# Layer 0's first-layer sums: two points in one VectorE operation, with interleaved pairs from ScalarE

## The chip, the cores and the metric

The kernel runs on one core of a Trainium2 chip. Its time is the device time of one execution in microseconds (us); lower is better. A core has TensorE (PE, the matmuls), VectorE (DVE), ScalarE (ACT), GpSimd (POOL) and SyncE (SP), each with its own queue of instructions, and 16 DMA engines that they share. All data here are float32.

## The reference

Four layers run one after the other on images of 512 channels; only layer 0 is touched by the change. It is an attention with 8 groups, whose keys are sampled at 64 learned offsets per group, and whose scores get a bias from a small network (the "continuous position bias"), for each pair of one of the 32x32 pixels and one of the 64 sampled points:

```python
pos = grid_q[:, :, None, :] - grid_kv[:, None, :, :]
bias = jnp.sign(pos) * jnp.log1p(jnp.abs(pos))
bias = jax.nn.relu(bias @ cpb_w1 + cpb_b1)       # 2 -> 128
bias = jax.nn.relu(bias @ cpb_w2 + cpb_b2)       # 128 -> 128
bias = (bias @ cpb_w3 + cpb_b3)                  # 128 -> 1
sim = jnp.einsum('bhid,bhjd->bhij', qh, kh) + bias
attn = jax.nn.softmax(sim, axis=-1)
```

There are 2 images x 8 groups x 64 points = 1024 points, and each has 1024 pixels. The first layer is separable: its input for pixel (y, x) has one part that depends on x alone and one that depends on y alone. So `relu(wx * X[x] + b + wy * Y[y])` is one sum of two rows of 32 numbers, spread over the 32x32 pixels and cut off at zero.

## The kernel before

Layer 0 (`layer0`, lines 192 to 963) works on eight tiles t of 128 (two groups of 64 points each). Inside a tile, 32 steps of four points: 256 steps i in all, one loop that is written out at build time. Four slots k make up a step. In each slot, one of the four parts of the second layer (32 of 128 outputs) is done for the step's four points.

What one step does, engine by engine:

- VectorE, `first(p)` (line 588; the operation is recorded at L599): the first layer of one point. A custom operation adds a row of 32 (the point's x part, from table `tab0`) and a column of 32 (its y part, from `tab1`) and cuts the sum off at zero; the result is 128 x 1024. It goes to `ring`, 11 buffers of one point each, three of their own (`h1`) and eight in the memory `wa` that later layers' weights use. Sums run `AHEAD = 7` points ahead of the step.
- PE, `second(i, h1s, part)` (L616): for each of the two halves of the pixels and the four points one matmul of 128 x 32 weights, which writes 32 of the 128 rows of a PSUM tile `z`. In the trace each such matmul has two records, 64 records to a step. The `z` tiles rotate through three buffers (`zt`, pool `att_ps_z`), which all other small PSUM tiles of the loop (`gpb`, `pk`, `pkv`, `pvo`, `po`, `pt`, `pa`, `pp`) share.
- ScalarE, in `second` (L625): bias and relu of `z` into an `h2` buffer: pool `h2q` (three buffers) for parts 1 and 3, `h2b` (three) for part 2, `h2p` or `h2j` (memory `bridge` and others) for part 0.
- VectorE, `joined` (L630): adds two parts into one, twice per step, in slots 1 and 3.
- GpSimd and SP: DMAs that add the joined parts of different rows into each other (L918 to L937), and the loads of the tables (L573).
- PE, `third` (L645) and `scores` (L653): every 16 steps, the third layer and the scores into `sim`.

The tables: `load_tabs(c)` (line 561) loads for a chunk c of 16 points the two 16x32 tables, one per axis, to all 128 partitions, from two buffers each (`tab0`, `tab1`). `scale_tab(c, ax)` (line 582) multiplies each with the first layer's weights, in place: on ScalarE at L587, on VectorE at L585 for the first chunk alone. In the loop that happens in steps with i % 4 = 1, the first axis in slot 0 and the second in slot 2, for the chunk that is needed a step later.

A chain of generators, `behind`, is advanced once in slots 1 and 3: the end of the tile before (`finish`: softmax, transposes, output projection), the offsets of the tile after next (`offsets`: on ScalarE 36 products at L408, reductions on VectorE at L414, a Gelu, L438, a Tanh), and the next tile's samples (`samples`: `gpb` L497, `near` L505 and L506, `wx` and `wy` L512 to L521, the matmuls `pk`, then `kvbd` L534, `pkv`, and `pvo` with the weights `ow`, which L492 loads together with `xt`, L488).

The order of the work is that of the program: `in_order` (line 57) ties each engine's instructions in layer 0 to the order in which they are written. A DMA stands on the queue that issues it. An instruction that waits holds up all that is behind it on its engine.

Of the kernel before, what the change touches and what calls it, by code (L numbers as in the profile page):

```python
# [19 lines left out]
P = 128  # L20
# [59 lines left out]
def kernel(ctx: ExitStack, tc: tile.TileContext, a: dict, out: bass.AP):  # L80
# [111 lines left out]
    def layer0(l0, fold_d, t2_b, o2_b):  # L192
# [6 lines left out]
        h2q = l0.enter_context(tc.tile_pool(name="att_h2q", bufs=3))  # L199
# [36 lines left out]
        ring = [one.tile([P, HW], F32, name=f"h1{k}") for k in range(3)]  # L236
        ring += [qkv2.rearrange("p k n -> p (k n)")[:, k * HW : (k + 1) * HW] for k in range(6)]
        ring += [proj2.rearrange("p k n -> p (k n)")[:, k * HW : (k + 1) * HW] for k in range(2)]
# [13 lines left out]
        ones = one.tile([P, P], F32, name="ones")  # L252
        nc.gpsimd.memset(ones, 1.0)
# [33 lines left out]
        def bias_weights():  # L287
            sort = h2b.tile([P, 7, P], F32, name="sort", tag="h2")
            row, below, w2t = [sort[:, k, :] for k in range(3)]
            perm = sort[:, 3:, :].rearrange("p b (r u) -> p b r u", u=32)  # L290
# [194 lines left out]
        def samples(t):  # L485
# [5 lines left out]
            ow = one.tile([P, C], F32, name="ow")  # L491
            nc.sync.dma_start(out=ow, in_=a["out_w"][pr * P : (pr + 1) * P, :])  # L492
# [18 lines left out]
            wx = one.tile([P, P], F32, name="wx")  # L511
# [15 lines left out]
            accumulate(pk[:, 1, :], [(wsum[:, 2:3].to_broadcast([P, P]), ident)])  # L527
            yield
            shift = one.tile([P, P], F32, name="shift")
# [12 lines left out]
            kq = one.tile([P, P], F32, name="kq")  # L542
# [3 lines left out]
            values = one.tile([P, P], F32, name="values")  # L546
# [16 lines left out]
        def load_tabs(c):  # L563

            t, rc = divmod(c, NCH)
            assert t in tables
            tabs_of[c] = []
            for ax in range(2):
                src = slog_d[t, ax].rearrange("(q r) i -> q r i", q=4)
                tab = two.tile([P, 16, 32], F32, name=f"tab{ax}")  # L570
                if 4 * c < LAST:
                    q, r = rc % 4, rc // 4 * 16
                    nc.sync.dma_start(out=tab, in_=src[q, r : r + 16, :].partition_broadcast(P))  # L573
                else:
                    q, r = rc % 2 * 2, 16 + (rc - 4) // 2 * 8
                    nc.sync.dma_start(
                        out=tab.rearrange("p (q r) i -> p q r i", q=2),
                        in_=src[q : q + 2, r : r + 8, :].partition_broadcast(P),
                    )
                tabs_of[c].append(tab)  # L580

        def scale_tab(c, ax):
            tab, w = tabs_of[c][ax], col("cpb_w1", ax)
            if c == 0:
                nc.vector.tensor_scalar(tab, tab, w, 0.0 if ax else col("cpb_b1"), ALU.mult, ALU.add)  # L585
            else:
                nc.scalar.activation(tab, tab, AF.Identity, bias=0.0 if ax else col("cpb_b1"), scale=w)  # L587

        def first(p):

            chunk, point = divmod(p, 16)
            if point == 0:
                tabs_of.pop(chunk - 1, None)
                if chunk + 1 < NT * NCH:
                    load_tabs(chunk + 1)
            tx, ty = tabs_of[chunk]
            h1 = ring[p % len(ring)]

            nc.vector._custom_dve(  # L599
                TENSOR_ADD_SAT,  # L600
                out=h1.rearrange("p (y x) -> p y x", x=W),
                in0=tx[:, point, :].unsqueeze(1).to_broadcast([P, H, W]),
                in1=ty[:, point, :].unsqueeze(2).to_broadcast([P, H, W]),
                s0=float(np.finfo(np.float32).max),
                s1=0.0,
            )
            return h1

        def second(i, h1s, part):

            z = zt([P, HW], "z")
            lo = BLOCK[part]
            for half in range(2):
                n = slice(half * HALF, (half + 1) * HALF)
                for point in range(4):
                    nc.tensor.matmul(  # L616
                        z[point * 32 : point * 32 + 32, n],
                        cpb_w2[:, lo : lo + 32],
                        h1s[point][:, n],
                        start=True,  # L620
                        stop=True,
                    )
            ring = h2q if part % 2 else h2b if part else h2j if i % (4 if i < LAST else 2) else h2p
            h2 = ring.tile([P, HW], F32, name="h2", tag="h2") if ring in (h2q, h2b) else next(ring)
            nc.scalar.activation(h2, z, AF.Relu, bias=b2h[:, part : part + 1])  # L625
            return h2
# [30 lines left out]
        def finish(t, sim):  # L657
# [4 lines left out]
            simb = one.tile([P, HW], F32, name="simb", tag="simb")  # L662
# [11 lines left out]
            at = one.tile([P, 8, P], F32, name="at", tag="simb")  # L674
# [42 lines left out]
        def finish_last(sim, eights, fours, right_sums, left_sums):  # L717
# [7 lines left out]
            simb = one.tile([P, HW], F32, name="simb", tag="simb")  # L725
# [161 lines left out]
        AHEAD = 7  # L887

        for p in range(AHEAD):
            h1s[p] = first(p)  # L890
        late_loads()
        for i in range(steps):
            for k, part in enumerate((1, 0, 3, 2)):
# [3 lines left out]
                if p < 4 * steps:  # L897
                    h1s[p] = first(p)
# [1373 lines left out]
```

## Time and profile before

| What | us |
|---|---|
| median of 3 runs | 3349.49 (3348.35 to 3349.53) |
| the profiled execution, its own time | 3353.46 |
| its span, first to last instruction | 3351.7 |
| layer 0's loop (first to last L616 record) | 59.6 to 1981.6 |
| VectorE busy from 60 to 1982 | 1848.57 |
| ScalarE busy from 60 to 1982 | 1412.19 |
| GpSimd busy from 60 to 1982 | 650.69 |
| L599 on VectorE, 1024 operations | 878.1 + 332.9 |
| L587 on ScalarE, 126 operations | 95.8 |

In the page, an instruction group is a line, an engine, an operation and the tiles it writes and reads; behind the bar stand its busy time, the mean of one in ns, and the engine's idle time before it with what ended most of that. Matmuls overlap in the pipeline and their ends are modelled, so a group's busy time there is not its cost; the distance between starts is. The chain of waits goes back from the last instruction to what released it, step by step. The sums in `wa` and those in their own buffers are two groups of the same line.

### The profile page before, as it was taken

What the parts mean: (1) busy time and instruction counts of PE and PEld (TensorE: products, weight loads), DVE (VectorE), ACT (ScalarE), POOL (GpSimd) and SP (SyncE); (2) the same over time, 40 slices, a digit from 0 to 9 for tenths busy, and PEclk for the clock granted to TensorE, in tenths of its full rate; (3) what the DMA queues carried; (4) which work ended last, traced back from release to release, by engine and by line L of the source; (5) the groups of instructions that cost most, each with busy time, mean ns of one, the idle gap of its engine ahead of it and who ended that gap; (6) DMA issues with size and microseconds to landing.
All of it is one profiled execution on the core that took longest, in us unless ns stands there. A gap on an engine that the chain in (4) does not pass through costs nothing.

```text
span 3351.7 us, 61808 instructions
## 1 busy us (share of the span) xinstructions
PE 3323.8 (99%) x24813; PEld 1611.7 (48%) x24813; DVE 2673.0 (80%) x3540; ACT 1805.5 (54%) x2774; POOL 676.7 (20%) x804
## 2 busy tenths in 40 slices
PE   9999999999999999999999999999999999999999
PEld 4333333332333332333333339999953443687777
DVE  6999999999999799999999976455446465665556
ACT  4866877877877577877877652122136245122221
POOL 0333333333333233333333310000000000000000
PEclk9999999999999999999999999999999999999999
DMA  5778787787787577787787751000100000000111
GB/s 166 157 161 166 153 168 156 152 166 153 158 167 155 103 162 155 159 169 152 158 166 157 161 135 58 14 8 14 52 0 14 26 29 20 7 7 3 30 32 36
DMA packets 142488, 343.97 MB, mean 103 GB/s; under 512 B 36464, under 2 KB 51440, under 8 KB 141424
## 3 DMA queue, kind: packets, MB, share of 16 engines
q0 software_dynamic: 68400, 231.26, 36.5%
q1 hardware_dynamic: 72496, 103.95, 10.7%
q8 instruction: 197, 3.23, 0.4%
q10 hardware_dynamic: 1296, 4.72, 0.4%
q14 instruction: 99, 0.81, 0.1%
HBM read 71.46 MB, written 10.83 MB: 25 GB/s over the span
## 4 chain that ended last, share of the span: by engine, by line
PE 82%; DVE 9%; issue 5%; DMA 2%; ACT 1%; POOL 1%; DVEq 0%; SPq 0%; POOLq 0%; ACTq 0%
PE z L616 38%; PE pma L135 6%; PE pw L1435 6%; PE pmb L135 5%; PE pmv L1435 4%; PE score L1614 3%; PE pv L1626 3%; DVE wa L599 3%; PE pm L1435 3%; PE score L1435 3%; PE pmt L1435 1%; PE ppr L1435 1%; DVE h L599 1%; DMA bridge<-h 1%; DVE bridge L630 1%
## 5 line engine op out<-in xcount | busy, mean ns | idle before, releaser
L616 PE MATMUL z<-wa,cpb_w 128*32 128x512 f32 x11904 | 1779.2, 593 | 5.8 <-ACT h L625 3.7
L625 ACT ACTIVATE h<-z,b2h 128x1024 f32<-128x1024 f32 x768 | 851.3, 1114 | 347.9 <-PE z L616 310.6
L616 PE MATMUL z<-h,cpb_w 128*32 128x512 f32 x4480 | 983.2, 593 | 1.6 <-ACT h L625 1.6
L616 PEld LDWEIGHTS z<-wa,cpb_w 128*32 128x32 f32 x11904 | 497.2, 110 | 888.2 <-issue 778.1
L599 DVE CUSTOM_DVE_ANT_1 wa<-tab,tab 128x1024 f32<-128x1024 f32 x744 | 878.1, 1216 | 1.3 <-PE z L616 1.1
L616 PEld LDWEIGHTS z<-h,cpb_w 128*32 128x32 f32 x4480 | 256.6, 110 | 328.6 <-issue 292.1
L599 DVE CUSTOM_DVE_ANT_1 h<-tab,tab 128x1024 f32<-128x1024 f32 x280 | 332.9, 1216 | 2.3 <-PE z L616 2.2
L630 DVE SCALAR_TENSOR_TENSOR h<-h,turn,h 128x1024 f32<-128x1024 f32 x256 | 326.8, 1276 | 4.3 <-ACT h L625 4.3
L625 ACT ACTIVATE bridge<-z,b2h 128x1024 f32<-128x1024 f32 x162 | 180.8, 1116 | 121.4 <-PE z L616 119.0
L927 POOL DMA_DIRECT2D bridge<-bridge x150 | 127.6, 850 | 547.2 <-DMA bridge<-h 510.5
L630 DVE SCALAR_TENSOR_TENSOR bridge<-bridge,turn,h 128x1024 f32<-128x1024 f32 x162 | 206.8, 1277 | 4.2 <-ACT bridge L625 4.2
L934 POOL DMA_DIRECT2D bridge<-h x161 | 163.4, 1015 | 213.2 <-DVE h L630 123.6
L1278 ACT COPY p<-pma 128x128 f32<-128x128 f32 x80 | 21.3, 266 | 334.7 <-PE pma L135 334.7
L1270 DVE TENSOR_TENSOR upper<-pma,p 128x256 f32<-128x256 f32 x80 | 33.7, 422 | 178.6 <-ACT p L1278 178.5
L1615 ACT ACTIVATE p<-score 128x512 f32<-128x512 f32 x256 | 130.0, 624 | 81.2 <-PE score L1614 79.6
L927 POOL DMA_DIRECT2D h2j<-h2j x90 | 76.2, 847 | 323.0 <-DMA h2j<-h 293.6
L1647 DVE TENSOR_TENSOR acc<-acc,p 128x1024 f32<-128x1024 f32 x96 | 111.0, 1217 | 19.4 <-ACT p L1615 19.3
L625 ACT ACTIVATE h2j<-z,b2h 128x1024 f32<-128x1024 f32 x94 | 105.0, 1117 | 37.9 <-PE z L616 37.3
L1614 PE MATMUL score<-q,k 64*128 64x512 f32 x512 | 120.7, 604 | 1.1 <-DVE gm L1191 1.1
L630 DVE SCALAR_TENSOR_TENSOR h2j<-h2j,turn,h 128x1024 f32<-128x1024 f32 x94 | 120.0, 1276 | 0.0
L1626 PE MATMUL pv<-p,vT 128*64 128x512 f32 x512 | 116.5, 598 | 0.0
L937 POOL DMA_DIRECT2D bridge<-h2j x90 | 111.9, 1244 | 2.6 <-issue 1.8
(458 smaller groups left out, 4379.8 us busy)
## 6 DMA issues: line engine op xcount, KB each, us to landing
bridge<-h POOLq DMA_DIRECT2D x161, 512.0 KB, 5.5
h2j<-h POOLq DMA_DIRECT2D x94, 512.0 KB, 5.9
bridge<-bridge POOLq DMA_DIRECT2D x159, 256.0 KB, 3.9
tab<-slog_d SPq DMA_DIRECT2D x128, 256.0 KB, 4.6
h2j<-h2j POOLq DMA_DIRECT2D x90, 256.0 KB, 3.2
bridge<-bridge POOLq DMA_DIRECT2D x150, 128.0 KB, 5.4
bridge<-bridge SPq DMA_DIRECT2D x90, 128.0 KB, 3.7
bridge<-h2j SPq DMA_DIRECT2D x90, 128.0 KB, 3.6
```

The source lines that it names most:

```text
L135: nc.tensor.matmul(pm, w, m, start=(k == 0), stop=(k == len(pairs) - 1))
L599: nc.vector._custom_dve(TENSOR_ADD_SAT, out=h1.rearrange("p (y x) -> p y x", x=W), in0=tx[:, point, :].unsqueeze(1).to_broadcast([P, H, W] ...
L616: nc.tensor.matmul(z[point * 32 : point * 32 + 32, n], cpb_w2[:, lo : lo + 32], h1s[point][:, n], start=True, stop=True,)
L625: nc.scalar.activation(h2, z, AF.Relu, bias=b2h[:, part : part + 1])
L630: nc.vector.scalar_tensor_tensor(h2, h2, turn[:, part // 2 : part // 2 + 1], parts.pop(part + 1), ALU.mult, ALU.add)
L927: nc.gpsimd.dma_start(out=own[0:P:2], in_=own[1:P:2], accum_op=ALU.add)
L934: nc.gpsimd.dma_start(out=joins[i - 1], in_=other, accum_op=ALU.add)
L937: nc.gpsimd.dma_start(out=joins[i - 3 - j][j:P:4], in_=joins.pop(i - 3)[2:P:4], accum_op=ALU.add)
L1435: nc.tensor.matmul(out, stationary(l, k), moving(r, k), start=start and k == 0, stop=k == nk - 1, skip_group_check=not start,)
L1614: nc.tensor.matmul(sc, ks[m][r, s * P : (s + 1) * P], qs[m][r, n], start=True, stop=True)
L1615: nc.scalar.activation(p[:, part], sc, AF.Exp, scale=64 ** -0.5)
L1626: nc.tensor.matmul(pv[half][part * 64 : part * 64 + 64], vt[s % 4][:, lo : lo + 64], lps[s, half][:, part, :], start=(s == 0), stop=(s == 7),)
```

## The change

Seven edits, all in layer 0:

1. `first(p)` makes two points, p and p + 1, in one operation of 128 x 2048, laid out by pixel row y, then point k, then x. It is called in slots 0 and 2 alone. The matmuls of the second layer read one point's half as 16 rows of 32 words, 64 words apart.
2. `ring` becomes six buffers of two points (twelve points): two of their own and four in `wa`. `AHEAD` is 8.
3. The second table's scaling writes to a new tile `pairs` (two buffers), in which the values of two points alternate: it reads `tab1` 32 words apart from one element to the next and writes in order. `tab1` keeps one buffer instead of two. The first table is scaled in place as before.
4. `h2q` has four buffers instead of three.
5. `ones` has no tile of its own: it is the eighth block of `sort`, and VectorE fills it instead of GpSimd.
6. `ow` shares the buffer of `xt` and `qpad` ("pixels"), and its load moves from the start of `samples` to behind the matmuls of `pk`.
7. Shared buffers: `wx` with `values`, `shift` with `kq`, and `simb` and `at` with `wy` and `products`.

```diff
-        h2q = l0.enter_context(tc.tile_pool(name="att_h2q", bufs=3))
+        h2q = l0.enter_context(tc.tile_pool(name="att_h2q", bufs=4))
...
-        ring = [one.tile([P, HW], F32, name=f"h1{k}") for k in range(3)]
-        ring += [qkv2.rearrange("p k n -> p (k n)")[:, k * HW : (k + 1) * HW] for k in range(6)]
-        ring += [proj2.rearrange("p k n -> p (k n)")[:, k * HW : (k + 1) * HW] for k in range(2)]
+        ring = [one.tile([P, 2 * HW], F32, name=f"h1{k}") for k in range(2)]
+        ring += [qkv2.rearrange("p k n -> p (k n)")[:, k * 2 * HW : (k + 1) * 2 * HW] for k in range(3)]
+        ring.append(proj2.rearrange("p k n -> p (k n)"))
...
-        ones = one.tile([P, P], F32, name="ones")
-        nc.gpsimd.memset(ones, 1.0)
...
-            sort = h2b.tile([P, 7, P], F32, name="sort", tag="h2")
+            sort = h2b.tile([P, 8, P], F32, name="sort", tag="h2")
+            ones = sort[:, 7, :]
+            nc.vector.memset(ones, 1.0)
...
-            ow = one.tile([P, C], F32, name="ow")
-            nc.sync.dma_start(out=ow, in_=a["out_w"][pr * P : (pr + 1) * P, :])
...
-            wx = one.tile([P, P], F32, name="wx")
+            wx = one.tile([P, P], F32, name="wx", tag="values")
...
             accumulate(pk[:, 1, :], [(wsum[:, 2:3].to_broadcast([P, P]), ident)])
+            ow = one.tile([P, C], F32, name="ow", tag="pixels")
+            nc.sync.dma_start(out=ow, in_=a["out_w"][pr * P : (pr + 1) * P, :])
             yield
-            shift = one.tile([P, P], F32, name="shift")
+            shift = one.tile([P, P], F32, name="shift", tag="kq")
...
-                tab = two.tile([P, 16, 32], F32, name=f"tab{ax}")
+                tab = (one if ax else two).tile([P, 16, 32], F32, name=f"tab{ax}")
...
             tab, w = tabs_of[c][ax], col("cpb_w1", ax)
+            to = tab
+            if ax:
+                tab = tab.rearrange("p (a k) i -> p a i k", k=2)
+                to = two.tile([P, 8, 32, 2], F32, name="pairs")
+                tabs_of[c][ax] = to
             if c == 0:
-                nc.vector.tensor_scalar(tab, tab, w, 0.0 if ax else col("cpb_b1"), ALU.mult, ALU.add)
+                nc.vector.tensor_scalar(to, tab, w, 0.0 if ax else col("cpb_b1"), ALU.mult, ALU.add)
             else:
-                nc.scalar.activation(tab, tab, AF.Identity, bias=0.0 if ax else col("cpb_b1"), scale=w)
+                nc.scalar.activation(to, tab, AF.Identity, bias=0.0 if ax else col("cpb_b1"), scale=w)
...
-            tx, ty = tabs_of[chunk]
-            h1 = ring[p % len(ring)]
+            tx, ty = tabs_of[chunk][0][:, point : point + 2, :], tabs_of[chunk][1][:, point // 2]
+            h1 = ring[p // 2 % len(ring)].rearrange("p (y k x) -> p y k x", k=2, x=W)
             nc.vector._custom_dve(
                 TENSOR_ADD_SAT,
-                out=h1.rearrange("p (y x) -> p y x", x=W),
-                in0=tx[:, point, :].unsqueeze(1).to_broadcast([P, H, W]),
-                in1=ty[:, point, :].unsqueeze(2).to_broadcast([P, H, W]),
+                out=h1,
+                in0=tx.unsqueeze(1).to_broadcast([P, H, 2, W]),
+                in1=ty.unsqueeze(3).to_broadcast([P, H, 2, W]),
...
-            return h1
+            return [h1[:, :, k, :] for k in range(2)]
...
-                        h1s[point][:, n],
+                        h1s[point][:, half * 16 : half * 16 + 16, :],
...
-            simb = one.tile([P, HW], F32, name="simb", tag="simb")
+            simb = one.tile([P, HW], F32, name="simb", tag="wy")
...
-        AHEAD = 7
-
-        for p in range(AHEAD):
-            h1s[p] = first(p)
+        AHEAD = 8
+
+        for p in range(0, AHEAD, 2):
+            h1s[p], h1s[p + 1] = first(p)
...
-                if p < 4 * steps:
-                    h1s[p] = first(p)
+                if p < 4 * steps and k % 2 == 0:
+                    h1s[p], h1s[p + 1] = first(p)
```

The lines of the profile before that the change touches keep their meaning in the changed kernel, whose line numbers are a few higher (L616 becomes L621, L599 L604, L625 L630, L630 L635, L587 L592).

More of the change, by code (lines that the diff above doesn't have):

```diff
@@ L287, in bias_weights @@
         def bias_weights():
-            sort = h2b.tile([P, 7, P], F32, name="sort", tag="h2")
+            sort = h2b.tile([P, 8, P], F32, name="sort", tag="h2")
+            ones = sort[:, 7, :]
+            nc.vector.memset(ones, 1.0)
             row, below, w2t = [sort[:, k, :] for k in range(3)]
-            perm = sort[:, 3:, :].rearrange("p b (r u) -> p b r u", u=32)
+            perm = sort[:, 3:7, :].rearrange("p b (r u) -> p b r u", u=32)
             few = one.tile([P, 28], F32, name="few")
@@ L541, in samples @@
             nc.tensor.matmul(pkv[:, 1, :], bd["vw"][:, pr, :], kv, start=True, stop=True)
-            kq = one.tile([P, P], F32, name="kq")
+            kq = one.tile([P, P], F32, name="kq", tag="kq")
             nc.scalar.copy(kq, pkv[:, 0, :])
@@ L545, in samples @@
             nc.scalar.mul(kqs[t], pkv[:, 0, :], s1q[:, pr : pr + 1])
-            values = one.tile([P, P], F32, name="values")
+            values = one.tile([P, P], F32, name="values", tag="values")
             nc.scalar.copy(values, pkv[:, 1, :])
@@ L673, in finish @@
             yield
-            at = one.tile([P, 8, P], F32, name="at", tag="simb")
+            at = one.tile([P, 8, P], F32, name="at", tag="wy")
             atv = at.rearrange("p i (g j) -> p (i g) j", j=NJ)
@@ L724, in finish_last @@
             project_out(pps[0], b, 0, range(2))
-            simb = one.tile([P, HW], F32, name="simb", tag="simb")
+            simb = one.tile([P, HW], F32, name="simb", tag="wy")
             for half, n in enumerate(halves):
```

## The prediction

> **What bounds the kernel now.** I read the groups of instructions first, then the chain of waits in order of time, then each engine's waits inside layer 0's loop (60 to 1982 us), then the timeline around the longest of them. From the page:
>
> ```profile
> PE 3323.8 (99%) x24813; PEld 1611.7 (48%) x24813; DVE 2673.0 (80%) x3540; ACT 1805.5 (54%) x2774; POOL 676.7 (20%) x804
> ...
> L616 PE MATMUL z<-wa,cpb_w 128*32 128x512 f32 x11904 | 1779.2, 593 | 5.8 <-ACT h L625 3.7
> ...
> L616 PE MATMUL z<-h,cpb_w 128*32 128x512 f32 x4480 | 983.2, 593 | 1.6 <-ACT h L625 1.6
> ...
> L599 DVE CUSTOM_DVE_ANT_1 wa<-tab,tab 128x1024 f32<-128x1024 f32 x744 | 878.1, 1216 | 1.3 <-PE z L616 1.1
> ```
>
> The columns after the bar are busy time, mean of one, and idle time before it. The loop is L616: 16384 matmul records, four at a time side by side. A busy matmul says nothing of pace, so take it from the chain:
>
> ```profile
> 210.64 109.87 PE z L616 x1024
> ```
>
> 1024 records in 109.87 us are 107.3 ns each (429 ns for four). All 16384 at that pace are 1758 us of the loop's 1922; the sim, transposing, projecting and sampling matmuls fill the rest. What PE lost is in its waits within the loop:
>
> ```profile
> PE z L616 <- ACT h L625: 5.3, 10, 0.6
> PE z L616 <- DVE kvbd L534: 2.1, 2, 1.6
> PE sim L645 <- DMA bridge<-bridge: 1.5, 2, 1.3
> ```
>
> That is 8.9 us in total. So the stretch that the change touches is paced by PE, though VectorE is busy for 1848.6 of its 1922 us. No edit that leaves PE's own work alone can win more than about 9 us here. The largest repeated stall, just after a sampling step (ScalarE, then PE):
>
> ```profile
> 690.08 0.31 ACT L505 ACTIVATE near<-ir,gp 128x32 f32<-128x32 f32 x1
> ...
> 690.65 0.30 ACT L505 ACTIVATE near<-ir,gp 128x32 f32<-128x32 f32 x1
> ...
> 691.21 0.71 ACT L587 ACTIVATE tab<-tab,pc 128x512 f32<-128x512 f32 x1
> 691.83 2.10 ACT L625 ACTIVATE h<-z,b2h 128x1024 f32<-128x1024 f32 x2
> ```
> ```profile
> 691.82 0.59 PE L616 MATMUL z<-wa,cpb_w 128*32 128x512 f32 x1
> 691.82 0.61 PE L616 MATMUL z<-h,cpb_w 128*32 128x512 f32 x3
> 692.97 1.50 PE L616 MATMUL z<-wa,cpb_w 128*32 128x512 f32 x12 [0.55 <-ACT h L625]
> ```
>
> PE starts a four 1.15 us after the last instead of 0.43: 0.72 us lost, because the scaling of the second table (L587) stands ahead of the relu that frees a PSUM buffer. The timeline has the same stall at 454.8, 932.2, 1436.2 and 1674.0.
>
> [...] one sum takes 1.216 us, two in a row 2.35, so the second adds 1.135. [...] the sum over k at L414 (448 elements, 64 words apart) takes 971 ns, and a contiguous reduction of 512 at L850 686. [...]
>
> **The change, part by part.**
>
> *Paired sums (L599).* 1024 operations become 512 of twice the length. Slope: the add L1647 (1024 elements, 1217 ns) less L1270 (256, 422) is 1.035 ns per element, so 2048 take 1216 + 1060 = 2276 ns alone and 1.135 + 1.060 = 2.195 us in a row, against 2.27 for two. Saved: 0.075 x 512 = 38 us of VectorE. Inputs and output still run through adjacent words or repeat one. PE covers it: per step VectorE needs 4 x 1.135 + 2 x 1.20 (two L630 in a row) = 6.94 us now and 2 x 2.195 + 2.40 = 6.79 then, PE 16 x 0.429 = 6.86. So it reaches PE only where VectorE was late. At 177.33 and 1240.79 a z waits for kvbd (L534), which reads pk out of its PSUM buffer behind late sums: 1.8 and 0.6 us between starts. I count both as gone: 2.4 us.
>
> *Twelve points, 8 ahead.* A sum overwrites points that the step before still reads, as now, so no wait is longer; the last points of a step are made one slot (1.7 us) earlier. Five waits on VectorE's sums at steps where the lead is near zero total 0.3 us. Gone: 0.3.
>
> *h2q from 3 to 4 buffers (parts 1 and 3).* ScalarE's relus wait for VectorE 9.0 + 7.0 + 4.8 us in the loop, and nearly all is covered by PE's buffers. What shows is after the offsets' L441: at 668.26 and four like it z starts 0.24 us late. Gone: 1.2.
>
> *Interleaved scaling (L587).* The second table (63 of the 126 L587; the first chunk is done on VectorE before the loop in idle time) now reads 32 words apart at every element and writes in order. The nearest ScalarE row is L408, whose 64 inputs lie 4 words apart: 406 ns. L505, 32 contiguous inputs, takes 309; at 0.83 ns an element (L1615's 512 in 624 ns against L678's 64 in 313 gives 0.69, L625's 1024 in 1114 against L1615 0.96; I take the middle) 64 would be 335. The hop costs 71 / 64 = 1.1 ns an element, so 0.57 us on 512. VectorE's row L414: at 1.035 ns 448 contiguous would take 620, so 0.78 ns, or 0.40 us. Below: zero[...]. It can't be a gain: as many elements. [...] I take 0.45. ScalarE is busy 1412 of 1922 us, so mostly PE covers it. Not covered: the stall shown above, five times 0.45 = 2.3 us. Before the exponentials, where pt holds one of three PSUM buffers, the relu after the table (573.21 to 574.33) has 0.32 us in hand before its z is wanted; seven times 0.13 = 0.9. After the Gelu table load (660 us) there are 0.6 us in hand: zero[...]. Sum +3.2[...].
>
> *One tab1 buffer.* Its load now waits for the scaling of the chunk before, in the step before. SP carries both table loads, then L931; landing takes 4.6 us (median) and the scaling comes three steps (20 us) later. Zero.
>
> *ow moved behind pk's matmuls, sharing xt's buffer.* SP now waits for PE there. Behind it stand L931 and, for L931, GpSimd's adds; SP already waits for landing DMAs before L931 (705 + 544 us between 200 and 1900 us). pk ends at 715.8 and ow is needed at 730.8; SP's lag of about 5 us (xt issued at 689.9, gpb matmuls at 684.7) and a landing of 5.9 leave 4 us. Zero; if one or two of eight land as late as 12.5 us, +2 each: 0 to +4.
>
> *Shared buffers (wx/values, shift/kq, simb/at with wy).* The former tenants are read a slot or more earlier in the same order: zero. The GpSimd memset of ones goes, and a VectorE one (about 0.2 us) stands in the wait before L301 (2.79 us idle): zero.
>
> *The second layer's matmuls* now read rows of 32 words, 64 apart. L343 reads its moving operand in four runs of 32 and its two records take 275 and 356 ns, the 275 of a contiguous 128x128 (L135). Value zero; but four side by side are not shown.
>
> Sum: -2.4 - 0.3 - 1.2 + 3.2 = -0.7 us. The span 3351.7 becomes 3351.0, the profiled execution 3353.46 (1.8 outside the span) 3352.8. That execution lies 4.0 above the runs' median; against 3349.49 the forecast is 3348.8. Ends: -8.9 (all loop stalls gone and a free hop)[...].
>
> **Rivals.**
> 1. *VectorE paces the loop.* For: 96% busy, and PE's busy time is modelled. Then all 38 us come: 3311. Against: PE's waits, 8.9 us. Part of it, all stalls gone and cheap hops, gives 3341.
> 2. *ScalarE's hop takes the place of what is won (slower).* Place: L587 behind L505 and behind the table loads; price: 5 to 19 us per us of extra length. It outweighs the 3.9 won from about 0.5 us (1.0 ns an element) and passes 0.2% from 0.9[...]. L408 and L414 speak for the smaller sizes.
> 3. *Strided moving operands slow PE.* Decides from 2 ns per four matmuls (4096 fours, 8 us); 1% gives 3367. L343 speaks against.
> 4. *The pairing doesn't merge*[...]: at 10% slower VectorE needs 7.2 us a step, and the loop follows it: about +60, 3410. The sums are contiguous; unlikely.
>
> **How the numbers follow.** What a measurement of this kernel can tell from no change is about 0.2% (6.7 us). Main forecast 0.62 (3343 to 3357); rival 1 0.17, mostly its partial form; rival 2 beyond 0.2% 0.12; rival 3 0.06; rival 4 0.03. Range 3341 to 3360 leaves out the full forms of 1 to 4, under 2 in 10. Faster 0.17, same 0.62, slower 0.21.
>
> **What would show it.** Right: L599 x512 near 2.28 us; VectorE busy 35 to 40 us less in the loop; the waits on kvbd gone; L587 in two lengths, the second 1.0 to 1.3 us; the stall near 692 longer by just that; fours still 429 ns apart. Wrong: fours further apart (rival 3), PE waiting for L599 (rival 4), waits of PE on ow, or a loop shorter by more than 9 us with PE's pace unchanged.

## The result, and the profile after

| | before | after |
|---|---|---|
| median, us | 3349.34 (14 runs, 3347.04 to 3352.35) | 3342.73 (14 runs, 3341.25 to 3345.43) |
| ratio to before | | 0.9981, 95% interval 0.9973 to 0.9988 |
| profiled execution: own time, span | 3353.46, 3351.7 | 3343.91, 3342.0 |
| first z of the loop starts | 59.57 | 57.36 |
| loop, first to last z | 1922.06 | 1910.28 |
| last z to the first pma (L135), the next stage | 38.13 | 42.83 |
| first pma to the end | 1331.9 | 1331.6 |

The change makes the kernel 6.6 us faster, 0.19%. The forecast was 3348.8. The stages say more than the total: the loop won 11.8 us, and the stretch behind it lost 4.7. (The 2.2 us before the first z go with no edit: in the runs below it starts at 56.4 to 59.4, in kernels of both families.) Each column of stages is one execution. That of before took 3353.46, more than any of its 14 runs, so the two traces lie 9.7 us apart where the medians lie 6.6 apart. The loop repeats well: it takes 1909.7 to 1910.3 in the changed kernel and in three runs below that keep its sums and its order (a_h2q3, a_load_act, a_hop_write).

The page of the changed kernel, busy times and the groups that answer to those shown of before:

```profile
PE 3319.8 (99%) x24813; PEld 1605.2 (48%) x24813; DVE 2640.9 (79%) x3029; ACT 1809.4 (54%) x2774; POOL 675.3 (20%) x803
...
L621 PE MATMUL z<-wa,cpb_w 128*32 128x512 f32 x10880 | 1191.9, 593 | 2.7 <-ACT h L630 2.7
...
L604 DVE CUSTOM_DVE_ANT_1 wa<-tab,pairs 128x2048 f32<-128x2048 f32 x340 | 776.4, 2284 | 3.1 <-PE z L621 2.6
...
L621 PE MATMUL z<-h,cpb_w 128*32 128x512 f32 x5504 | 609.5, 593 | 0.7 <-ACT h L630 0.7
L604 DVE CUSTOM_DVE_ANT_1 h<-tab,pairs 128x2048 f32<-128x2048 f32 x172 | 392.7, 2284 | 1.7 <-PE z L621 1.5
```

A pair takes 2284 ns, and there are 340 + 172 = 512. VectorE is busy 32 us less (2673.0 to 2640.9), 63 ns for each pair. The chain of waits in order of time has the same piece as before:

```profile
206.59 109.87 PE z L621 x1024
```

1024 records in 109.87 us again: PE's own pace has not changed by a nanosecond, and rows of 32 words, 64 apart, as its moving operand cost nothing here. In the summary of that chain, PE's share rises from 82% to 96% and VectorE's falls from 9% to 1%. First before, then after:

```profile
PE 82%; DVE 9%; issue 5%; DMA 2%; ACT 1%; POOL 1%; DVEq 0%; SPq 0%; POOLq 0%; ACTq 0%
```
```profile
PE 96%; DVE 1%; issue 1%; ACT 1%; DMA 1%; SPq 0%; POOL 0%; DVEq 0%; ACTq 0%; POOLq 0%
```

The waits of PE in the loop (57 to 1968 us; us in total, times, longest) have shrunk to one line, from the three shown of before:

```profile
PE z L621 <- ACT h L630: 3.3, 5, 0.7
```

Gone are VectorE's kvbd and the DMA that ends the join of rows ahead of a third layer. What is left are the five stalls at the second table's scaling (ScalarE, then PE):

```profile
684.83 0.83 ACT L592 ACTIVATE pairs<-tab,pc 128x512 f32<-128x512 f32 x1
685.55 2.11 ACT L630 ACTIVATE h<-z,b2h 128x1024 f32<-128x1024 f32 x2
```
```profile
683.28 2.76 PE L621 MATMUL z<-wa,cpb_w 128*32 128x512 f32 x24
686.71 1.07 PE L621 MATMUL z<-wa,cpb_w 128*32 128x512 f32 x8 [0.67 <-ACT h L630]
```

**Where the loop's time came from.** The loop has 1024 groups of z (256 steps of four slots). I took the time from the start of each to the start of the next in both traces, and added the differences by step and slot over the eight tiles:

| place in the tile | after less before, us |
|---|---|
| step 4, slot 0, before the third layers there (two of seven sites make 3.6) | -3.8 |
| step 20, slot 3, behind the third layers of step 20 (0.82 at three sites) | -2.5 |
| step 18, slot 3, at L441 (0.66 to 0.70, five sites) | -3.4 |
| steps 15 and 27, slot 3, at kvbd | -2.2 |
| step 21, slot 3, at the second table's scaling (0.12, five sites) | +0.6 |

That is 11.3 of the 11.8. The first two rows are waits for the joins (the DMAs that add rows ahead of a third layer), 6.3 us; what is printed for them before is 1.5.

**The way from VectorE to the third layer.** A third layer needs rows that DMAs have added together. The last of these transfers (L937, now L942) is issued on GpSimd's queue behind another (L934, now L939), which waits for a sum of VectorE (L630, now L635). One case before, VectorE and GpSimd, then PE:

```profile
669.19 1.27 DVE L630 SCALAR_TENSOR_TENSOR h<-h,turn,h 128x1024 f32<-128x1024 f32 x1
```
```profile
670.76 0.86 POOL L934 DMA_DIRECT2D bridge<-h  x1 [0.38 <-DVE h L630]
671.30 1.17 POOL L937 DMA_DIRECT2D bridge<-bridge  x1
```

VectorE's sum ends at 670.46, L934 goes out 0.30 later, L937 at 671.30. Its transfer takes 6.38 us and lands at 677.68; the third layer has begun at 676.87, and one quarter of PE must wait (the last of the sixteen sim records begins at 679.04). The other three go on with the next z (from 678.62), and the loss comes at the end of that step, where the quarters are in line again: 0.83 us, of which the waits print nothing. The largest case lies one third layer further on, where GpSimd's queue had first waited for an earlier transfer:

```profile
795.38 1.04 PE L645 MATMUL sim<-bridge,w 128*32 128x512 f32 x6
797.71 1.48 PE L645 MATMUL sim<-bridge,w 128*32 128x512 f32 x9 [1.29 <-DMA bridge<-bridge]
```

From this slot's z to the next 7.79 us pass, and 5.46 after, so the place costs 2.33. The wait is printed as 1.29: it is counted from the modelled end of the records before it, and the quarter that could not start at all (six of the first eight records ran) isn't counted. The same place after:

```profile
789.12 1.90 PE L650 MATMUL sim<-bridge,w 128*32 128x512 f32 x16
790.95 0.70 PE L658 MATMUL sim<-x,kqs 128*128 128x512 f32 x1
```

Means over the fifteen third layers, in us; the first two columns count from the start of slot 1 two steps earlier, and the margin is from the landing to the third layer's first record:

| kernel | VectorE's sum ends | last transfer issued | its length | margin |
|---|---|---|---|---|
| before | 5.65 | 7.23 | 6.60 | 0.28 |
| after | 4.51 | 5.95 | 6.24 | 1.69 |

So VectorE, back to back in these steps, is 1.1 us less behind, and the last transfer is issued 1.3 us earlier. At the five of the fifteen that lie like the first case, the sum ends 6.74 to 6.78 us after the slot's start instead of 8.45 to 8.48.

Not all of the 6.3 us come this way. At the two sites in step 4 that make 3.6 of it, the queue was held by its own transfers: VectorE's sum of the largest case had ended at 785.96, but L927 had waited for an earlier transfer, and L934 stood behind it.

```profile
787.91 0.86 POOL L927 DMA_DIRECT2D bridge<-bridge  x1 [3.70 <-DMA bridge<-h]
788.47 1.20 POOL L934 DMA_DIRECT2D bridge<-h  x1
```

The run a_single below keeps everything of the change but the pairing. Its sums end as late after the slot's start at these two sites as before (4.31 and 4.13 us), yet the queue is free for the sum, and PE loses nothing at either. The same place, where L940 is what L934 was:

```profile
785.66 0.86 POOL L940 DMA_DIRECT2D bridge<-h  x1 [1.05 <-DVE h L636]
```

b_h2q4 and b_scale01, which start from the kernel before, lose time at both places as it does. So these 3.6 us belong to something in the change other than the pairing. Which edit put the queue ahead there is open.

### The profile page after: what moved, and what is told of

It reads as the page before. It is cut to its first block, busy times and chain, and to the rows that moved or that the text cites. A ratio compares the mean times of both kernels' runs of the same rounds, so it can differ in the third digit from the quotient of the medians.

```text
span 3342.0 us, 60958 instructions
## 1 busy us (share of the span) xinstructions
PE 3319.8 (99%) x24813; PEld 1605.2 (48%) x24813; DVE 2640.9 (79%) x3029; ACT 1809.4 (54%) x2774; POOL 675.3 (20%) x803
## 4 chain that ended last, share of the span: by engine, by line
PE 96%; DVE 1%; issue 1%; ACT 1%; DMA 1%; SPq 0%; POOL 0%; DVEq 0%; ACTq 0%; POOLq 0%
PE z L621 52%; PE pma L135 6%; PE pw L1440 6%; PE pmb L135 5%; PE pmv L1440 4%; PE score L1619 3%; PE pv L1631 3%; PE pm L1440 3%; PE score L1440 3%; PE ppr L1440 1%; PE pmt L1440 1%; PE sim L650 1%; PE pf L135 1%; PE pp L710 1%; PE pma L1343 1%
## 5 line engine op out<-in xcount | busy, mean ns | idle before, releaser
L621 PE MATMUL z<-wa,cpb_w 128*32 128x512 f32 x10880 | 1191.9, 593 | 2.7 <-ACT h L630 2.7
L630 ACT ACTIVATE h<-z,b2h 128x1024 f32<-128x1024 f32 x768 | 851.1, 1113 | 331.0 <-PE z L621 301.7
L604 DVE CUSTOM_DVE_ANT_1 wa<-tab,pairs 128x2048 f32<-128x2048 f32 x340 | 776.4, 2284 | 3.1 <-PE z L621 2.6
L621 PEld LDWEIGHTS z<-wa,cpb_w 128*32 128x32 f32 x10880 | 346.5, 110 | 809.3 <-issue 712.4
L621 PE MATMUL z<-h,cpb_w 128*32 128x512 f32 x5504 | 609.5, 593 | 0.7 <-ACT h L630 0.7
L604 DVE CUSTOM_DVE_ANT_1 h<-tab,pairs 128x2048 f32<-128x2048 f32 x172 | 392.7, 2284 | 1.7 <-PE z L621 1.5
L621 PEld LDWEIGHTS z<-h,cpb_w 128*32 128x32 f32 x5504 | 175.1, 110 | 407.9 <-issue 362.7
L635 DVE SCALAR_TENSOR_TENSOR h<-h,turn,h 128x1024 f32<-128x1024 f32 x256 | 327.1, 1278 | 5.5 <-ACT h L630 5.5
L630 ACT ACTIVATE bridge<-z,b2h 128x1024 f32<-128x1024 f32 x162 | 180.8, 1116 | 119.0 <-PE z L621 119.0
L932 POOL DMA_DIRECT2D bridge<-bridge x150 | 127.5, 850 | 539.5 <-DMA bridge<-h 517.5
L635 DVE SCALAR_TENSOR_TENSOR bridge<-bridge,turn,h 128x1024 f32<-128x1024 f32 x162 | 207.0, 1278 | 4.3 <-ACT bridge L630 4.3
L939 POOL DMA_DIRECT2D bridge<-h x161 | 158.4, 984 | 247.0 <-DVE h L635 151.8
L630 ACT ACTIVATE h2j<-z,b2h 128x1024 f32<-128x1024 f32 x94 | 104.9, 1116 | 41.5 <-PE z L621 41.5
L635 DVE SCALAR_TENSOR_TENSOR h2j<-h2j,turn,h 128x1024 f32<-128x1024 f32 x94 | 120.1, 1278 | 0.0
L942 POOL DMA_DIRECT2D bridge<-bridge x90 | 111.1, 1235 | 0.2 <-issue 0.2
```

Of the source, the lines that this page charges most:

```text
L604: nc.vector._custom_dve(TENSOR_ADD_SAT, out=h1, in0=tx.unsqueeze(1).to_broadcast([P, H, 2, W]), in1=ty.unsqueeze(3).to_broadcast([P, H, 2, ...
L621: nc.tensor.matmul(z[point * 32 : point * 32 + 32, n], cpb_w2[:, lo : lo + 32], h1s[point][:, half * 16 : half * 16 + 16, :], start=True, ...
L635: nc.vector.scalar_tensor_tensor(h2, h2, turn[:, part // 2 : part // 2 + 1], parts.pop(part + 1), ALU.mult, ALU.add)
L932: nc.gpsimd.dma_start(out=own[0:P:2], in_=own[1:P:2], accum_op=ALU.add)
L939: nc.gpsimd.dma_start(out=joins[i - 1], in_=other, accum_op=ALU.add)
L942: nc.gpsimd.dma_start(out=joins[i - 3 - j][j:P:4], in_=joins.pop(i - 3)[2:P:4], accum_op=ALU.add)
```

## Experiments

All times in us; the ratio is to the kernel before on the same chip. Names that begin with a_ start from the changed kernel, with b_ from the one before.

| run | median | ratio (95% interval) | loop | last z to pma |
|---|---|---|---|---|
| a_single | 3349.93 | 1.0001 (0.9993 to 1.001) | 1916.7 | 41.5 |
| a_h2q3 | 3343.56 | 0.9983 (0.9976 to 0.999) | 1910.1 | 41.4 |
| b_h2q4 | 3351.32 | 1.0007 (0.9999 to 1.0015) | 1921.8 | 38.1 |
| b_third3 | 3340.90 | 0.9976 (0.9966 to 0.9986) | 1912.2 | 38.1 |
| b_scale01 | 3349.81 | 0.9995 (0.9987 to 1.0004) | 1919.3 | 38.1 |
| a_third3 | 3344.30 | 0.9982 (0.9975 to 0.9988) | 1909.5 | 43.9 |
| a_ring_shift | 3346.38 | 0.9991 (0.9983 to 1.0) | 1912.8 | 38.1 |
| a_skip | 3357.25 | 1.0028 (1.0018 to 1.0039) | 1927.9 | 38.1 |
| a_load_act | 3340.49 | 0.9971 (0.9958 to 0.9983) | 1910.0 | 38.1 |
| a_skip_scale01 | 3355.72 | 1.0018 (1.0011 to 1.0025) | 1925.9 | 38.1 |
| a_load_act_scale01 | 3337.06 | 0.9959 (0.9945 to 0.9972) | 1907.1 | 38.1 |
| a_hop_write | 3342.95, one run | | 1909.7 | 41.3 |

The median of before was 3350.91 beside a_third3, b_scale01, a_load_act and a_load_act_scale01, and 3349.4 beside the others.

### What gives the gain: the pairing, or the buffers?

**a_single**: all buffers of the change, but two operations for each pair.

```diff
-            nc.vector._custom_dve(
-                TENSOR_ADD_SAT,
-                out=h1,
-                in0=tx.unsqueeze(1).to_broadcast([P, H, 2, W]),
-                in1=ty.unsqueeze(3).to_broadcast([P, H, 2, W]),
+            for k in range(2):
+                nc.vector._custom_dve(
+                    TENSOR_ADD_SAT,
+                    out=h1[:, :, k, :],
+                    in0=tx[:, k, :].unsqueeze(1).to_broadcast([P, H, W]),
+                    in1=ty[:, :, k].unsqueeze(2).to_broadcast([P, H, W]),
...
```

> The changed kernel with all its buffers, its interleaved table and its ring, but each pair's sum as two VectorE operations of 1024 elements instead of one of 2048. Theory (the shorter VectorE work itself gives the gain, through waits that it ends last): VectorE is busy some 32 to 38 us more, 60 to 75 ns for each of 512 pairs; the waits before the kvbd products return (2 us), the loop's h2 waits of ScalarE for VectorE double again (11 to about 20 us), and the time goes to 3346 to 3349. Rival (the buffers, a fourth h2q and twelve points of room, give the gain, and the pairing is beside the point): VectorE is as much busier, the time stays within 1 us of 3342.7.

The time is that of before, 0.9 us beyond the theory's range, and VectorE is busy 2673.3 us, as before. Its waits of PE in the loop (57 to 1970 us):

```profile
PE z L622 <- ACT h L631: 3.3, 5, 0.7
PE z L622 <- DVE kvbd L534: 2.5, 3, 1.9
PE sim L651 <- DMA bridge<-bridge: 0.6, 1, 0.6
```

Against the changed kernel, the loop is 6.4 us longer: by groups, 3.2 at kvbd (steps 15, 25 and 27) and 2.9 at the joins (steps 4 and 20; none of it at the two large sites). The theory holds: the 32 us of VectorE pay, though only a fifth of them. Everything else in the change gives nothing in the time that the interval could show: its loop is 5.4 us shorter than before, and its end 3.3 longer. The 5.4 are 3.4 at L441 and 3.5 at the joins of step 4, less 1.4 lost at the scaling and at kvbd in step 25. So of the 6.3 us that the joins gave up, the pairing accounts for 2.9.

**a_h2q3** and **b_h2q4**: the fourth h2q buffer taken from the changed kernel, and given to the one before.

```diff
-        h2q = l0.enter_context(tc.tile_pool(name="att_h2q", bufs=4))
+        h2q = l0.enter_context(tc.tile_pool(name="att_h2q", bufs=3))
```

> The changed kernel with three h2q buffers again instead of four. Theory (the fourth h2q buffer takes the stalls of TensorE in the groups after L441, five of 0.59 us, 3.0 us in all): they return and the time goes to 3345.5 (3344.5 to 3346.5). Rival (the earlier VectorE alone took them, since the buffer comes free with the h2 sum that stands behind the first layer's sums on VectorE): no change, 3342.7 within 1.

```diff
-        h2q = l0.enter_context(tc.tile_pool(name="att_h2q", bufs=3))
+        h2q = l0.enter_context(tc.tile_pool(name="att_h2q", bufs=4))
...
-            wx = one.tile([P, P], F32, name="wx")
+            wx = one.tile([P, P], F32, name="wx", tag="values")
...
-            shift = one.tile([P, P], F32, name="shift")
+            shift = one.tile([P, P], F32, name="shift", tag="kq")
...
```

> The kernel before with a fourth h2q buffer and nothing else of the change (wx shares the tile of values, and shift that of kq, to make the room). Theory (the fourth buffer takes the stalls after L441): 3.0 us less than before, 3346.3 (3345.3 to 3347.3), with the kvbd waits (2.4 us) still there. Rival (only a shorter VectorE takes them): no change, 3349.3 within 1.

The rival is right for a_h2q3: the changed kernel doesn't need the fourth buffer. The kernel before wins nothing by it; its median is even 1.9 us higher, more than the rival allowed, in an interval that includes no change. Yet in b_h2q4 the stalls at L441 are gone (2.9 us less in step 18). The waits of PE say where they went:

```profile
PE z L616 <- ACT h L625: 2.7, 5, 0.6
PE z L616 <- DVE kvbd L534: 2.1, 2, 1.7
PE sim L645 <- DMA bridge<-bridge: 1.8, 3, 1.1
```

There are five waits for ScalarE's h instead of ten, and one more for a join. By groups, step 20, two steps after L441, is 2.6 us longer: PE comes there earlier, the joins don't. What PE gained at one wait it lost at the next.

### Is it the joins by which VectorE holds PE?

**b_third3**: in the kernel before, the wide third layers move two groups of z later. No work is taken away, and VectorE keeps its 1024 sums.

```diff
-                if k == 1 and 0 <= due < LAST and due % 16 == 0:
+                if k == 3 and 0 <= due < LAST and due % 16 == 0:
```

> The kernel before with one word changed: the fifteen wide third layers, with the scores behind them, are issued in slot 3 of their step instead of slot 1, two groups of z (3.5 us) later; VectorE keeps its 1024 single sums. Theory (the late VectorE reaches TensorE through the last join's transfer, which in the kernel before lands on average only 0.28 us ahead of its third layer and after it in seven of fifteen, while the changed kernel has 1.69 us): with 3.5 us more of room nearly every third layer runs its 1.31 us unstalled, 6.6 us less in the sum of fifteen, and without any pairing the time goes to about 3343.5 (3342.5 to 3345). Rival (the joins' delay merely shows the wait that VectorE would make somewhere else anyway): the waits for the transfer go and others of the same size come, 3348 to 3350.

It is faster than expected, and as fast as the changed kernel at least. The margin of the last transfer goes from 0.28 us (negative at six of the fifteen; the expectation says seven) to 4.08, and all fifteen third layers take their unstalled 2.13 us from the last z ahead of them to the next (4.15 with scores). The waits (57 to 1970 us):

```profile
PE z L616 <- DVE kvbd L534: 1.6, 1, 1.6
PE z L616 <- ACT h L625: 0.4, 1, 0.4
```

So the joins' waits need no faster VectorE to go. But the edit did more than the question asked, for what follows a third layer moved with it: the scaling after step 21 no longer stands behind the operations on `near` (0.71 to 0.17 us, five times: 2.7), the stalls at L441 went, and new ones of 0.27 us came in seven tiles. The loop's 9.9 us are, by groups, 2.3 at steps 4 to 6 and 7.7 at steps 18 to 23, with 0.1 lost elsewhere. What PE lost at the joins before, 6.7 us from start to start, is gone; the rest is the balance of L441, the scaling and the new stalls.

**b_scale01** takes the scalings alone:

```diff
-                if i % 4 == 1 and k % 2 == 0 and i // 4 + 1 in tabs_of:
-                    scale_tab(i // 4 + 1, k // 2)
+                if i % 4 == 1 and k < 2 and i // 4 + 1 in tabs_of:
+                    scale_tab(i // 4 + 1, k)
```

> The kernel before with the two scalings of a table in slots 0 and 1 of their step instead of 0 and 2, and nothing else. In the run of it with the third layers in slot 3, the stalls of 0.71 us after step 21 went to 0.17 besides what the joins won; this edit shows them alone. Theory (most of the 8.5 us of that run are the joins', and these five stalls are 2.7 to 3.5 us of it at most): 3346.3 (3345.5 to 3348). Rival (the stalls at the scalings were most of it and the joins little): 3344 or less. Second rival (as with the fourth h2 buffer, an earlier TensorE meets the late joins and gives it back): 3348.5 to 3350.

The five stalls shrink from 0.71 to 0.10 us, 3.0 in all, and 0.8 comes back at kvbd in step 25; the loop is 2.8 us shorter. The time falls by 1.1, with an interval that includes no gain. It doesn't decide between the theory and the second rival: 3349.81 lies in the rival's range, but 0.9995 of 3349.34 is 3347.7, just inside the theory's. The first rival is out. So the scalings alone do not make b_third3, and most of its 8.5 us stays with the joins and L441.

**a_third3** makes the same move in the changed kernel. It asks whether pairing still pays where the joins have room.

> The changed kernel with the fifteen wide third layers, and what follows from them, issued in slot 3 instead of slot 1: the edit that took the kernel before from 3349.4 to 3340.9. Theory (pairing and the later third layers take away the same waits for the joins, and only what the later start of the following work does to ScalarE's scalings, up to 2.7 us, is new): 3340.5 (3339.5 to 3342), so that pairing, worth 6.6 us with the third layers in slot 1, is worth about nothing with them in slot 3. Rival (the two add up, since VectorE's shorter work pays by itself): 3334 (3333 to 3336).

No gain at all: 0.9982, as the changed kernel has. Its loop is 0.8 us shorter than the changed kernel's; beside b_third3, pairing shortens the loop by 2.7 us (1912.2 to 1909.5) and lengthens the end by 5.8 (38.1 to 43.9). Whether it is worth anything in sum with the third layers in slot 3 can't be told (0.9982 against 0.9976, the intervals overlap); that the two add up is excluded. No run holds back the load of the next section as well. My figure of 3340.5 left out that load, which lengthens the end of the changed kernel and not that of b_third3.

### The 4.7 us behind the loop

The chain of waits at the end of the changed kernel's loop, from 1955 us on:

```profile
1963.90 0.02 POOLq L939
1963.92 0.49 issue
1964.41 10.63 DMA bridge<-h
1975.04 0.04 issue
1975.08 2.38 PE sim L650 x6
```

The last join's transfer takes 10.63 us. Before, the same one took 4.53 (1978.40 to 1982.93). SP's queue shows what else began:

```profile
1961.43 2.01 SPq L119 DMA_DIRECT2D wa<-in_mlp_w  x4
```

These four transfers are the 4 MB load of the next weights into `wa`, 3 us ahead of the join; before, it began at 1982.27, after the loop. The ring of six has 512 pairs go round, and the last two (510 and 511) fall on the two buffers outside `wa`: so `wa` is free one step earlier, and the load runs at once.

**a_ring_shift** turns the ring, so that the last pairs lie in `wa`.

```diff
-        ring = [one.tile([P, 2 * HW], F32, name=f"h1{k}") for k in range(2)]
+        ring = [proj2.rearrange("p k n -> p (k n)")]
         ring += [qkv2.rearrange("p k n -> p (k n)")[:, k * 2 * HW : (k + 1) * 2 * HW] for k in range(3)]
-        ring.append(proj2.rearrange("p k n -> p (k n)"))
+        ring += [one.tile([P, 2 * HW], F32, name=f"h1{k}") for k in range(2)]
```

> The changed kernel with the six pair buffers of its ring in another order: proj2, the three of qkv2, then the two of their own, so that the last step's two pairs (510 and 511, places 0 and 1 of six) lie in the weight tile again. Theory: the 4.7 us that the end of the loop lost (from the last z to the first pma: 38.1 us before, 42.8 after) come from the 4 MB load of mlp_w1 starting before the last join's transfer is issued (1961.4 against 1964.4), which then takes 10.6 us instead of 4.5; with the weight tile read to the last step the load starts after the loop's end, the join lands in about 4.5 us, the stretch goes back to about 38 and the time to about 3338 (3337 to 3339.5). Rival: the last join is late because of the faster VectorE or of the joins' own queue, and the load has nothing to do with it: the stretch stays at 42 to 43 and the time at 3342.7. Second rival: the load, started later, is late for the next stage's first use of the weights: the stretch is short but the stage after it begins later, 3342 or more.

The end does what the theory says: the load starts at 1972.80, the join lands after 4.52 us, the stretch is 38.13. The time doesn't follow, since the first pairs now lie in `wa` as well and the loop starts badly (57 to 300 us):

```profile
PE z L621 <- DVE wa L604: 2.7, 2, 2.5
```

In the profiled execution (3343.5) that and the later first z (59.37) about cancel the 4.7. The median is 2.9 higher still, and the runs spread over 7 us; why, is open.

**a_skip** keeps the ring's start and passes over one place twice on the way.

```diff
-            h1 = ring[p // 2 % len(ring)].rearrange("p (y k x) -> p y k x", k=2, x=W)
+            h1 = ring[(p // 2 + (p >= 800) + (p >= 900)) % len(ring)].rearrange("p (y k x) -> p y k x", k=2, x=W)
```

> The changed kernel with its own ring order, and one place of the ring passed over twice, at points 800 and 900, so that the first pairs still lie in the two buffers of their own and the last step's pairs lie in the weight tile; ten points of room instead of twelve for a moment at each. Theory: the first z begins as early as in the changed kernel (57.4 us), the load of mlp_w1 starts after the loop's end as in the kernel before, the stretch from the last z to the first pma is about 38 us instead of 42.8, and the time 3338.5 (3337.5 to 3339.5). Rival (the start of the load is not what counts, and the shorter stretch of the run with the turned ring came with its later loop): 3342.5 or more.

A miss, by my own edit. First z at 56.4 and an end of 38.13 as hoped, but each skip makes a pair wait for a buffer that PE still reads, and then PE for the pair:

```profile
PE z L621 <- DVE wa L604: 8.9, 3, 3.9
PE z L621 <- DVE h L604: 4.5, 1, 4.5
PE z L621 <- ACT h L630: 3.3, 5, 0.7
```

The loop is 17.6 us longer. It shows what the room for twelve points is for: with ten and `AHEAD` 8, two times five pairs cost that.

**a_load_act** leaves the ring alone and moves the load to ScalarE's queue, behind the loop's last h.

```diff
-        (w1s,) = load_w(wa, "wa", [a["mlp_w1"]])
+        (w1s,) = load_w(wa, "wa", [a["mlp_w1"]], nc.scalar)
```

> The changed kernel with one edit: the four transfers of mlp_w1 are issued on ScalarE's queue, where they stand behind the last h of the loop, instead of SP's, where nothing stands before them. The ring is that of the changed kernel, so the weight tile is free as early. Theory (the load that starts 3 us ahead of the last join's issue makes its transfer 10.6 us instead of 4.5): the load now starts at the loop's end, the join lands in about 5 us, the stretch from the last z to the first pma goes from 42.8 (41.2 to 42.8 in the runs so far) to about 38.1 as in the runs whose load was held back by the ring, the loop and its start stay as they are, and the time is 3338.5 (3337.5 to 3340). Rival (what counted was only that the runs with another ring came late to that place, or the issues on ScalarE cost what the join wins): 3341.5 or more.

```profile
1954.75 12.88 PE z L621 x120
1967.63 3.63 PE pp L710 x8
1971.26 1.85 PE sim L650 x12
1973.11 1.07 PE sim L658 x2
```

In the chain the join's transfer has gone (it took 4.52 us), PE runs through, and the stretch is 38.13 with a loop as in the changed kernel. By its ratio, 0.9971 against 0.9981, it takes 3.3 us; the two intervals overlap, so the size of this step rests on the traces.

### The scaling on ScalarE

**a_skip_scale01** and **a_load_act_scale01**: the edit of b_scale01, on top of a_skip and of a_load_act.

> The kernel of the run with the two skips, and the two scalings of a table on ScalarE in slots 0 and 1 of their step instead of 0 and 2. Theory (the stall of 0.83 us in the group after step 21, once in each of five tiles, comes from the interleaved scaling standing behind the operations on near in slot 2): the five stalls go, 4.2 us at most, 3 taken, and the time is 3 us below that of the run with the two skips, about 3335.5 (3334 to 3337). Rival (ScalarE is as late with the scaling in slot 1, before the same operations, and the stall only moves to another group): no change against the run with the two skips.

> The kernel of the run with the load on ScalarE's queue, and the two scalings in slots 0 and 1 of their step. In the run with skips and this edit the five stalls of 0.83 us after step 21 went to 0.11 and a tile of 32 steps took 235.6 us instead of 236.3. Theory: the two edits have nothing in common and add up: 3.5 us less than the run with the load alone, 3335 (3334 to 3337), the fastest of all. Rival (they meet at ScalarE, or the pace of the tile is set elsewhere once both are gone): within 1 us of the run with the load alone.

In the first, under the price of the skips, the five stalls go from 0.83 to 0.11 us and a tile of 32 steps from 236.3 to 235.6; the time is 1.5 us lower, half of what I expected, with intervals that overlap. In the second the loop is 2.9 us shorter than in a_load_act, and the time lower by 3.4 (3340.49 to 3337.06, same chip). From its first to its last z no wait of PE is listed at all. It is the fastest kernel of the study, 0.9959 of before. The loop gained as much in b_scale01 (2.8); that the median fell by 1.1 there and by 3.4 here is within the intervals, and no difference between the two is shown.

**a_hop_write** interleaves on the writing side.

```diff
-                tab = tab.rearrange("p (a k) i -> p a i k", k=2)
-                to = two.tile([P, 8, 32, 2], F32, name="pairs")
-                tabs_of[c][ax] = to
+                tab = tab.rearrange("p (a k) i -> p a k i", k=2)
+                tabs_of[c][ax] = two.tile([P, 8, 32, 2], F32, name="pairs")
+                to = tabs_of[c][ax].rearrange("p a i k -> p a k i")
```

> The changed kernel with the interleaving on the other side of ScalarE's scaling: it reads the second table in order and writes every second word, where the changed kernel reads with a hop of 32 words and writes in order. Theory (the hop costs 0.24 ns for each of 512 elements, on the read side: 832 ns against about 710 in the kernel before): the operation takes 0.70 to 0.75 us. Rival (it is the two-row order itself, on either side): 0.83 us, or more if a written word of 4 bytes alone costs more. The time as in the changed kernel, within a microsecond or two, either way.

The scaling by its two tables (minimum, median, maximum in ns), in the changed kernel and in this one:

```profile
L592 ACT ACTIVATE pairs<-tab,pc x63: 817/832/869, 72.3 to 1923.0; 128x512 f32<-128x512 f32 x63
```
```profile
L592 ACT ACTIVATE pairs<-tab,pc x63: 777/793/828, 73.0 to 1923.1; 128x512 f32<-128x512 f32 x63
```

In order on both sides it was 713 (before, median of the second table). So the hop comes to 119 ns on the reading side and 80 on the writing side; neither theory nor rival is right by itself. (Before wrote in place, these two write to another tile; no run separates that.)

## Why the prediction was right, and where it was wrong

The result lies in the range, just below the 3343 to 3357 of the main forecast (whose upper end rests on no trace of before), and the signs of four terms were right. But 3342.73 is 6.1 us from 3348.8, and that it lies in the range at all is in part luck: errors of both signs met. Without the 4.7 us behind the loop, which I hadn't foreseen either, it would lie below 3341 (a_load_act has 0.9971, and that share of 3349.34 is 3339.6). Step by step:

- *Paired sums.* 2284 ns for a pair against 2276 worked out; VectorE saved 32 us against 38. Right: with one operation instead of two, VectorE is busy 63 ns less for each pair. That the wait on kvbd goes was right in mechanism and size: 2.2 against 2.4, and in a_single it returns.
- *"So it reaches PE only where VectorE was late."* True of the pairing, but I looked for such places only among the waits that name VectorE. The join waits name a DMA, and I gave them nothing, though that DMA stands on GpSimd's queue behind VectorE's sum. This is the step that failed: the joins were worth 6.3 us. The pairing gave 2.9 of them, for a_single has these back with the single sums; the other 3.4 stay gone in a_single, so they came with another edit, and which is open. b_third3 takes all of them away without a faster VectorE.
- *The limit of 9 us.* I listed a loop shorter by more than that as what would prove me wrong, and it is 11.8 shorter. The listed waits are counted from modelled ends of matmuls; a printed 1.29 was 2.33 from start to start, and a quarter of PE that lags is not listed at all. The best run's loop is 15.0 shorter than before. As a bound, 8.9 was too small by 6 us at least.
- *h2q.* Mis-sized and mis-attributed: the groups at L441 won 3.4 us, not 1.2, and the fourth buffer isn't needed for it (a_h2q3). Nor is the pairing (a_single): in the changed kernel either of the two does, and in the kernel before the buffer alone.
- *Interleaved scaling.* Mechanism and place right, size wrong: 0.12 us for a scaling instead of 0.45, and 0.6 us in the loop instead of 3.2. L408 at 4 words and L414 on VectorE (1.1 and 0.78 ns an element, estimated from their 406 and 971 ns) were poor neighbours for a hop of 32 words that alternates between two rows (0.23 measured).
- *Twelve points.* "No wait is longer" failed outside the loop. I followed the ring at its start and in the middle, and not which buffers its last step holds: the 4.7 us behind the loop come from there. That room itself is needed was shown by a_skip. Of the 0.3 us that I counted as gain at the sums, 0.2 came (steps 10 and 12).
- *Moving operands, ow, the one tab1 buffer, shared buffers.* No loss, as said: 429 ns for four as before, and PE waits for none of them. Whether one of these edits freed GpSimd's queue at the two sites of step 4 isn't known.

Of the rivals, the first in its partial form (3341) described best what happened, VectorE's lateness taken from PE, but for another reason than I had: VectorE doesn't pace the loop, it delays kvbd and transfers that PE then meets. The second, slower, needed four times the hop's cost or more.

## What to carry to other kernels

A wait that names a DMA is to be followed to the instruction that its queue stood behind: a late engine can hold another through a transfer (here the sum ended 1.1 us earlier and the last transfer was issued 1.3 us earlier), and then room in time (here one word, moving a consumer by half a step: b_third3, 8.5 us) gives as much as making the engine faster (6.6). When buffers are laid out anew, ask of the last round as well as the first which of them it leaves free, for what is waiting to be loaded there starts by itself, and the last transfer that matters can take longer beside it (10.63 us here instead of 4.53). A wait can also vanish for another reason than the one that was meant, so take the meant edit back alone (a_single) before it is given the whole gain. And stalls in a row aren't added up: with the first one gone, PE met the next (b_h2q4: 2.9 us won, 2.6 lost two steps on).

## What the runs showed of the hardware

- One 512 KB transfer of GpSimd's queue at the end of the loop takes 4.5 us in before, a_ring_shift and a_load_act. In the changed kernel, where a 4 MB load was issued on SP's queue 3 us ahead of it, it takes 10.63; in a_third3, which has the same ring, 11.6.
- In a_skip, after an idle time of 4.5 us, PE's granted clock was 0.59 on average from 1551 to 1555 us and 1.00 from 1555 to 1560. By stretch (columns: busy time and count of PE, PEld, DVE, ACT, POOL, then the granted clock, and DMA's share and GB/s):

```profile
1545.90:1550.40 4.50, 0.07 (x4) 0.00 (x0) 4.50 (x4) 2.00 (x7) 2.57 (x3) 1.00 0.92 218
1551.00:1555.00 4.00, 4.00 (x28) 1.32 (x24) 0.51 (x1) 1.11 (x1) 1.45 (x2) 0.59 0.81 152
```

  The eight fours from 1550.46 on took 5.13 us to the next start at 1555.59, instead of 3.43 (eight times 0.429), so that stall cost its own time and about 1.7 us more. What brings the lower clock about was not shown.
- ScalarE reading one word in 32, alternating between two rows, took 0.23 ns an element more than the scaling in order (832 ns on 512 in the changed kernel against 713 before), and writing every second word took 0.16 more (793 in a_hop_write).
